# Two attention blocks on one core: the next sample's second norm on ScalarE alone, and two kinds of weight loads issued by ScalarE at set places

## The chip, the core and the metric

The kernel runs on one core of a Trainium2 chip. The time is that of one execution on the device in microseconds (us). Engines are named as the profile names them: PE is TensorE (matrix products), PEld its loading of weights, DVE is VectorE, ACT is ScalarE, POOL is GpSimd and SP is SyncE, which here only issues transfers (DMAs).

## What is computed

The input x has 8 samples of 512 channels by 1024 positions, all in float32. Two layers follow each other, and the eight samples are independent. Cut to what matters:

```python
# layer 0: group norm over 32 groups of channels, 8 heads of 64 channels
h = group_norm(x, norm_w, norm_b)
q, k, v = qkv_w @ h + qkv_b                    # each 512 x 1024 for a sample
o = softmax(q^T k * 64**-0.5) v                # for each head
x = x + proj_w @ o + proj_b
# layer 1: a norm over the whole sample, one head of 512 channels
n = (x - mean(x)) * rsqrt(var(x) + 1e-5) * gamma + beta
q, k, v = wq @ n + bq, wk @ n + bk, wv @ n + bv
x = x + wo @ (v softmax(q^T k * 512**-0.5)^T) + bo
```

## The kernel before

**Stages of a sample.** The loop over b (the 8 samples) is written out in full. For one sample PE runs these stages: the products for V of layer 0 (`make_v`, tile ps_v); the half of q and k that is still open (ps_s_qk, ps_o_qk and ps_l_qk, by `pairs_qk_twice`); the scores and values of 4 pairs of heads (s and ps_o); the first half of q and k of the *next* sample (ps_q, ps_k); the projection (ps_p); then in `attention1` the q stage (ps_q again, with the combined weights of q and k of layer 1), V of layer 1 (ps_s_v, ps_o_v and ps_l_v, by `make_v_twice`), the scores (ps_s, ps_l), and the values (ps_o at L1466, then ps_s_two and ps_o_two at L1588). The first norm of sample b+1 is thus computed while sample b is in layer 0. To hold fewer buffers its result is not kept: near the end of sample b, x of b+1 is loaded once more and normed a second time from the same scale and shift. This is the "second norm" of the title.

**Strassen's scheme.** Every large product is done by quarters in Winograd's form of Strassen's scheme (`strassen`, L414): seven products of quarters in place of eight. Sums of quarters of one side are called S1 to S4, those of the other T1 to T4. Each group of seven uses two accumulators in PSUM, one called line and one called single. Between the products, ACT copies the line (L425), and DVE adds what the results need. Where the kernel applies the scheme twice (`by_two_steps`, L526), it needs the S sums of a quarter of a weight as well. These "second-step sums of weights" are made once, written to DRAM, and later read back in two loads of 512 KB each by the class `WeightTwice` (L504 and L505): `qk_twice` for layer 0 (7 samples, b > 0) and `wvo_twice` for V of layer 1 (all 8 samples).

**The order of the work.** PE, ACT and DVE run in the order in which the program is written. A stage is a list of steps, and `at_steps` runs "hooks" after chosen steps, so that a hook's number sets where its instructions stand between the stage's own, on each engine. SP's order is not written by hand: the framework puts its transfers where it finds them due. A program counts DMAs with eight semaphores in turn, so in each queue a DMA also waits for the one eight places before it. Tiles of 512 KB come from one pool of 36 buffers (L88).

**Around the second norm.** `normed` (L366) works on 128x512 pieces, four chunks of channels in each of two halves of the positions. Odd chunks are done by ACT (`activation` with scale and bias, L372), even ones by DVE (`tensor_scalar`, L374), so a sample's second norm has four of each. It is called from `at_values` (L1719): half 0 at hook 8, half 1 at hook 9 of the values stage of layer 1. Steps 0 to 9 of this stage are `four_of(0)` and `four_of(1)` (L1554, five products each); then come the seven steps of `two_of` (L1577), whose products alternate between a line (ps_s_two) and a single (ps_o_two). After each of these DVE adds the accumulator to a sum c (L1594), and only then may PE write that accumulator again. In the order of DVE, around hooks 8 and 9, stand the quotients (L1482 and L1485), the four pieces of the norm (L374), the first two additions of c, and then in turn one of the four differences T1 to T4 of the next sample's x (`Combined.make`, L400, called t_again) and one addition of c.

**Around the loads.** `WeightTwice("wvo1")` stands at the head of `attention1` (L1219) and `WeightTwice("qk13")` at the head of V of layer 0 (L897). Both are issued by SP. In SP's order the first load of wvo_twice stands between two groups of eight small transfers (L1069, 64 KB each), which spread the reciprocals of the softmax sums over the partitions; the second stands behind the second group and a load of w_wvo. DVE multiplies by these reciprocals (`divide`, L957) ahead of the four sums T1 to T4 for the projection (L1007) and of the projection's own additions (L1180). The first load of qk_twice stands between loads of x and stores of out, the second behind these stores.

**The q stage** (`make_q`, L1234) has the steps of two groups of Strassen's scheme, one after the other in turn. On ACT it has six copies of a line (L425) and eight scaled results (L1242); two of the latter wait for the vector c, which the hook at 5 makes (`norm.untaken`, L354 to L357).

Of the kernel before, what the change touches and what calls it, by code (L numbers as in the profile page):

```python
# [46 lines left out]
P = 128  # L47
C = 512
NC = C // P
# [16 lines left out]
def two_attention_blocks(  # L66
# [17 lines left out]
    nc = tc.nc  # L84
# [112 lines left out]
    stored = {}  # L197
# [106 lines left out]
    class Norm:  # L304
# [58 lines left out]
            nc.vector.tensor_tensor(bias, made["v_b"], bias, ALU.subtract)  # L363
            return bias

        def normed(self, hs, halves=range(2)):  # L366
            for half in halves:
                for cc in range(NC):
                    h, x = piece(hs, cc, half), piece(self.xs, cc, half)
                    scale, shift = self.scale[:, cc : cc + 1], self.shift[:, cc : cc + 1]  # L370
                    if cc % 2:
                        nc.scalar.activation(h, x, AF.Identity, bias=shift, scale=scale)  # L372
                    else:
                        nc.vector.tensor_scalar(h, x, scale, shift, ALU.mult, ALU.add)  # L374
# [121 lines left out]
    class WeightTwice:  # L496
# [3 lines left out]
        def __init__(self, name, make=None):  # L500
            tiles = [flat(tile2(f"{name}_twice_{n}")) for n in range(2)]
            key, self.tiles = f"{name}_twice", tiles
            if make is None:
                nc.sync.dma_start(tiles[0], stored[key][:, : 8 * P])  # L504
                nc.sync.dma_start(tiles[1], stored[key][:, 8 * P :])  # L505
                return
            for n, pair in enumerate(PAIRS):
                for i, (a, _) in enumerate(pair):
                    sums_a(self.quarters(a, make), tiles[n][:, i * 4 * P : (i + 1) * 4 * P])
            stored[key] = dram.tile([P, 16 * P], FP, tag=key, name=f"stored_{key}")  # L510
            for n in range(2):
                nc.sync.dma_start(stored[key][:, n * 8 * P : (n + 1) * 8 * P], tiles[n])
# [85 lines left out]
    def at_steps(steps, hooks):  # L598

        n = -1  # L600
        for n, _ in enumerate(steps):
            for hook in hooks.get(n, []):
                hook()
        assert n >= max(hooks, default=-1)
# [219 lines left out]
    def pairs_qk_twice(w, twice_a, oc, bs, twice_b, qs, ks, b):  # L824

        pairs = [[tile2(f"{n}_{name}_0_{b}_{oc}") for name in "qk"] for n in ["c11", "c12"]]
        for i, ts in enumerate([qs, ks]):
            (c11, c22), (c12, c21) = ([p[i][:, half, :] for half in range(2)] for p in pairs)
            ts[oc], ts[oc + 2] = [c11, c12], [c21, c22]

        def bias(i, n):
            at = [V_BQ0, V_BK0][i] + oc + 2 * n
            return vec[:, at : at + 1]

        of = both_of(w)
        parts = twice_a.all(of)

        def multiply(bank, n, x, y, start):
            for i, (a, v) in enumerate(PAIRS[n]):
                nc.tensor.matmul(  # L840
                    bank[:, i * 2 * P : (i + 1) * 2 * P], parts[a][x], twice_b[v][y],
                    start=start and i == 0, stop=True, skip_group_check=True,
                )

        def multiply_line(i, bank, a, v, start):
            for k in range(2):
                nc.tensor.matmul(  # L847
                    bank, of(i, a)[:, k, :], bs[v][:, k, :], start=start and k == 0, stop=k == 1,
                    skip_group_check=True,
                )  # L850

        def at(n, r, t):
            return pairs[n][r][:, :, t * 2 * P : (t + 1) * 2 * P]

        return by_two_steps(multiply, multiply_line, pairs, at, bias, f"qk_0_{b}")
# [29 lines left out]
    def layer0(bs, qs, ks, b, norm_next):  # L885
# [3 lines left out]
        w = next_weight().parts[0]  # L889
        hooks = {}  # L890
# [3 lines left out]
            hooks[8] = [lambda cc=cc: norm_next.of_channels(cc) for cc in range(NC)]  # L894
        twice_b = {}
        if b > 0:
            twice_a = WeightTwice("qk13")  # L897
            for n, part in enumerate(["B21", "T1", "B22", "T4"]):
                hooks.setdefault(n, []).append(lambda part=part: twice_b.update(
                    {part: quarters_b(bs[part], f"{part}_twice_0_{b}")}  # L900
                ))
# [63 lines left out]
        w = next_weight()  # L965
# [10 lines left out]
        hooks = {8: [lambda: score(0)], 9: [lambda: score(1)]}  # L976
# [12 lines left out]
        if b == 0:  # L989
            hooks[9].append(lambda: WeightTwice("qk13", both_of(w)))  # L990
            at_steps(together(*pairs_qk(w, 1, bs, qs, ks, b)), hooks)
        else:
            hooks = {n + 10: more for n, more in hooks.items()}
            at_steps(pairs_qk_twice(w, twice_a, 1, bs, twice_b, qs, ks, b), hooks)
        xs = load_x(b, nc.sync)
        norm = norm1(xs, b)

# [137 lines left out]
        if not last:  # L1135
# [3 lines left out]
            hooks = {  # L1139
                0: [lambda n=n: combine2(n, 0) for n in range(1, 5)],  # L1140
                1: [lambda: folded(end)],
                3: [
                    lambda: sum_couple(couple, [room("sum", g) for g in range(2)]),
                    lambda: copy_couple(couple, 0), lambda: copy_couple(couple, 1),
                    lambda: one_over_couple(couple, 0),
                ],
                5: [lambda: held_couple(0)],
# [10 lines left out]
        later = []  # L1158
# [39 lines left out]
        w = next_weight().parts[0]  # L1198
# [7 lines left out]
    def attention1(xs, norm, b, at_values):  # L1206
# [9 lines left out]

        qs = quarters_of(f"q_1_{b}")
        w = next_weight().parts[0]
        twice_w = WeightTwice("wvo1")  # L1219
        combine, later = Combined(f"1_{b}"), []  # L1220
        combine.take(xs)
        bs = combine.parts
# [11 lines left out]
        def make_q(c):  # L1234
# [25 lines left out]
            6: [lambda: halve_b("T1")],  # L1260
            7: [lambda: halve_b("B22")],
            8: [lambda: halve_b("T4")],
            5: [norm.untaken, lambda: later.pop(0)(), lambda: later.pop(0)()],
        })
        bias = norm.bias()

# [5 lines left out]
        def finish_q(n):  # L1272
            q_parts[f"S{n}"] = tile2(f"s{n}_q_{b}")
            finish(q_parts, a21, n)

        at_steps(make_v_twice(w, twice_w, bs, twice_b, v_pairs, f"v_1_{b}"), {
            **{2 * n + 3: [lambda n=n: finish_q(n)] for n in range(1, 5)}, 13: [lambda: halve_a("S1")],
        })

# [354 lines left out]
    with tc.manual_schedule(engines={PE, ACT, DVE}):  # L1634
# [72 lines left out]
        for b in range(B):  # L1707
            if 0 < b < B - 1:
                ahead = [norm0(load_x(b + 1, nc.sync), b + 1)]
            xs, norm, qs, ks = layer0(bs, qs, ks, b, ahead[0] if b + 1 < B else None)  # L1710
            at_values = {}
            if b + 1 < B:

                again, combine_next = ahead[0], Combined(f"again_{b}")

                def load_again():
                    again.xs = load_x(b + 1, nc.sync)

                at_values = {  # L1719
                    2: [load_again], 8: [lambda: again.normed(again.xs, [0])],  # L1720
                    9: [lambda: again.normed(again.xs, [1])],
                    10: [lambda: combine_next.take(again.xs)],
                    **{n + 10: [lambda n=n: combine_next.make(n)] for n in range(1, 5)},
                }
                bs = combine_next.parts
            attention1(xs, norm, b, at_values)
# [412 lines left out]
```

## Time and profile before

| what | value |
|---|---|
| median of 3 runs (lowest to highest) | 2853.42 us (2852.35 to 2854.21) |
| the profiled execution's own time | 2854.65 us |
| span of the profile | 2852.4 us, granted PE clock 0.999 |
| PE busy | 2835.5 us (99%) |
| DVE busy | 2109.9 us (74%) |
| ACT busy | 1107.3 us (39%) |
| POOL busy | 220.1 us (8%) |
| DMA moved | 228.83 MB, mean 80 GB/s |
| loads of wvo_twice | 16 of 512 KB, median 5.1 us to landing |
| loads of qk_twice | 14 of 512 KB, median 6.4 us to landing |
| L374, DVE, 128x512 | 540 ns each |
| L372, ACT, 128x512 | 804 ns each |

Every figure but the first row is from one profiled execution. A busy PE is modelled: the end of a matrix product is computed, not observed. The profile's text lists waits as "who <- whom: us in total, times, longest us". A line of the timeline has the start, the duration, the engine, the source line, the operation, the tiles as out<-in, how many instructions are merged (x4), and in square brackets the idle time of the engine before it with what ended it. SPq and ACTq are the instruction queues of SP and ACT, on which DMAs are issued. A steady sample takes about 350 us; sample b = 1 begins at 413 us, when PE starts on its ps_v.

### The profile page before, as it was taken

Reading aid. Unit: us, or ns where it says so; the run is one execution under the profiler, and the core shown is the slowest. Engines: PE = TensorE matmul, PEld = TensorE weight load, DVE = VectorE, ACT = ScalarE, POOL = GpSimd, SP = SyncE. Lnnn points to the kernel's source line nnn. Section 1 sums busy time; section 2 is a strip of 40 time slices with the busy share of each in tenths; the row PEclk is TensorE's granted clock in tenths of the full one; section 3 lists DMA queues with packets and bytes.
Section 4 is the critical chain, followed back from the end, with each engine's and each line's share of the span. In section 5 each row is a group of like instructions: output and inputs, shape, how many; then the busy total and the mean of one; then the engine's idle time right before and its main releaser. Section 6 shows DMA issues by size and latency. Waiting matters only on the chain.

```text
span 2852.4 us, 37942 instructions
## 1 busy us (share of the span) xinstructions
PE 2835.5 (99%) x15200; PEld 1500.8 (53%) x15200; DVE 2109.9 (74%) x2863; ACT 1107.3 (39%) x1536; POOL 220.1 (8%) x172
## 2 busy tenths in 40 slices
PE   9999999999999999999999999999999999999999
PEld 5434765347643476435673356733557335573365
DVE  6686696866967768776677777777767777767867
ACT  3462324623256231553325523265232652326432
POOL 0000210002000030000300003000030000300011
PEclk9999999999999999999999999999999999999999
DMA  8512132121322213223132131322212222122001
GB/s 288 178 42 88 52 111 93 42 89 53 111 93 49 84 68 97 92 46 107 56 107 73 43 107 56 107 79 49 96 63 100 79 60 87 61 74 68 23 1 38
DMA packets 82567, 228.83 MB, mean 80 GB/s; under 512 B 20432, under 2 KB 21200, under 8 KB 75984
## 3 DMA queue, kind: packets, MB, share of 16 engines
q1 hardware_dynamic: 82240, 226.31, 24.7%
q8 instruction: 121, 1.98, 0.3%
q14 instruction: 62, 0.51, 0.1%
q10 hardware_dynamic: 144, 0.02, 0.0%
HBM read 153.16 MB, written 30.67 MB: 64 GB/s over the span
## 4 chain that ended last, share of the span: by engine, by line
PE 93%; DVE 5%; issue 0%; SPq 0%; ACT 0%; DMA 0%; POOL 0%; DVEq 0%; POOLq 0%
PE s L918 16%; PE ps_o L937 15%; PE ps_q L611 10%; PE ps_v L626 7%; PE ps_o L1466 7%; PE ps_p L611 6%; PE ps_s L1307 6%; PE ps_l L1323 4%; PE ps_k L611 3%; PE ps_l_v L626 3%; PE ps_s L1323 3%; PE ps_l_qk L847 3%; PE ps_s_v L868 2%; PE ps_s_qk L840 2%; PE ps_o_v L868 2%; PE ps_s_two L1588 1%
## 5 line engine op out<-in xcount | busy, mean ns | idle before, releaser
L777 ACT ACTIVATE p<-s 128x1024 f32<-128x1024 f32 x512 | 524.0, 1025 | 322.1 <-PE s L918 310.4
L779 DVE TENSOR_TENSOR acc<-acc,p 128x1024 f32<-128x1024 f32 x384 | 469.3, 1222 | 98.6 <-ACT p L777 85.8
L937 PE MATMUL ps_o<-p,v 64*64 64x512 f32 x4096 | 528.7, 589 | 0.0
L937 PEld LDWEIGHTS ps_o<-p,v 64*64 64x64 f32 x4096 | 156.6, 133 | 282.8 <-issue 278.4
L918 PE MATMUL s<-q,k 64*64 64x512 f32 x2304 | 298.5, 591 | 0.0
L918 PE MATMUL s<-c_q,c_k 64*64 64x512 f32 x1792 | 233.0, 590 | 0.0
L339 POOL TENSOR_TENSOR rstd<-rstd,minus_half 128x4 f32<-128x4 f32 (+1 forms) x16 | 19.8, 1240 | 2108.4 <-DVE rstd L338 2108.4
L918 PEld LDWEIGHTS s<-q,k 64*64 64x64 f32 x2304 | 86.3, 133 | 162.6 <-issue 156.6
L1466 PE MATMUL ps_o<-t_p,s_v 128*128 128x512 f32 x384 | 168.2, 594 | 0.0
L918 PEld LDWEIGHTS s<-c_q,c_k 64*64 64x64 f32 x1792 | 67.7, 133 | 126.3 <-issue 114.9
L779 DVE TENSOR_TENSOR acc<-p,p 128x1024 f32<-128x1024 f32 x64 | 77.9, 1217 | 73.8 <-ACT p L777 73.8
L1311 ACT COPY p<-ps_s 128x512 f32<-128x512 f32 x96 | 56.1, 585 | 195.3 <-PE ps_s L1307 193.9
L1466 PEld LDWEIGHTS ps_o<-t_p,s_v 128*128 128x128 f32 x384 | 72.3, 190 | 94.5 <-issue 94.5
L1307 PE MATMUL ps_s<-s_q,t 128*128 128x512 f32 x256 | 120.3, 592 | 0.0
L425 ACT COPY u_v<-ps_v 128x512 f32<-128x512 f32 x48 | 28.1, 586 | 231.6 <-PE ps_v L626 225.3
L1296 ACT ACTIVATE p<-p,factor 128x512 f32<-128x512 f32 (+1 forms) x112 | 86.8, 782 | 78.6 <-DVE p L1333 48.2
L611 PE MATMUL ps_p<-t_p,w_p 128*128 128x512 f32 x256 | 114.5, 596 | 2.8 <-DVE u_p L1180 2.0
L1333 DVE TENSOR_TENSOR p<-ps_s,p 128x512 f32<-128x512 f32 x88 | 60.0, 688 | 76.7 <-PE ps_s L1323 76.5
L611 PE MATMUL ps_q<-t,w_wqk 128*128 128x512 f32 x256 | 116.0, 597 | 0.0
L425 ACT COPY u_q<-ps_q 128x512 f32<-128x512 f32 x75 | 43.6, 581 | 177.1 <-PE ps_q L611 177.1
L1063 DVE RECIPROCAL inv<-inv 128x512 f32<-128x512 f32 x28 | 93.7, 3346 | 22.9 <-ACT inv L786 22.9
L1333 DVE TENSOR_TENSOR p<-ps_l,p 128x512 f32<-128x512 f32 x104 | 70.9, 688 | 47.5 <-PE ps_l L1323 47.5
(438 smaller groups left out, 4817.0 us busy)
## 6 DMA issues: line engine op xcount, KB each, us to landing
x<-in_x SPq DMA_DIRECT2D x92, 512.0 KB, 7.0
w_qk<-stored_qk SPq DMA_DIRECT2D x14, 1792.0 KB, 7.2
inv<-inv SPq DMA_DIRECT2D x248, 64.0 KB, 2.0
w_wqk<-stored_wqk SPq DMA_DIRECT2D x8, 1792.0 KB, 7.4
fold<-acc SPq DMA_DIRECT2D x56, 256.0 KB, 3.1
w_wvo<-stored_wvo SPq DMA_DIRECT2D x8, 1792.0 KB, 7.5
out<-x SPq DMA_DIRECT2D x28, 512.0 KB, 3.2
w_v<-stored_v SPq DMA_DIRECT2D x7, 1792.0 KB, 7.1
```

The costliest lines, as they stand in the source:

```text
L611: nc.tensor.matmul(bank, w[a][:, k, c * P : (c + 1) * P], bs[b][:, k, :], start=fresh and k == 0, stop=k == 1, skip_group_check=True,)
L626: nc.tensor.matmul(bank[:, u * 2 * P : (u + 1) * 2 * P], bs[b][:, k, n * P : (n + 1) * P], w[a][:, k, :], start=fresh and u == k == 0, sto ...
L777: nc.scalar.activation(p, s, AF.Exp, scale=factor)
L779: nc.vector.tensor_tensor(acc, first, p, ALU.add)
L868: nc.tensor.matmul(bank[:, (2 * i + u) * P : (2 * i + u + 1) * P], twice_b[v][y][:, u * P : (u + 1) * P], parts[a][x], start=start and i = ...
L918: nc.tensor.matmul(s[cols, j, :], ks[pair][k0 // HALF][rows, k0 % HALF : k0 % HALF + HD], qs[pair][g][rows, :], start=True, stop=True,)
L937: nc.tensor.matmul(o[cols, half, :], vs[kt][rows, c0 : c0 + HD], p[rows, j, :], start=kt == 0, stop=kt == NT - 1,)
L1063: nc.vector.reciprocal(invs[g], invs[g])
L1307: nc.tensor.matmul(bank, bs[v][:, k, t * P : (t + 1) * P], q_parts[a][:, k, :], start=a == "A11" and k == 0, stop=k == 1, skip_group_check ...
L1323: nc.tensor.matmul(bank[:, u * 2 * P : (u + 1) * 2 * P], v[y][:, u * P : (u + 1) * P], a[x], start=start and u == 0, stop=True, skip_group ...
L1333: nc.vector.tensor_tensor(at(r, t), bank, at(r, t), ALU.add)
L1466: nc.tensor.matmul(bank, v_parts[kt // 2][a][:, kt % 2, c * P : (c + 1) * P], p_parts[kt // 2][b][:, kt % 2, cols], start=fresh and kt == ...
```

## The change

Three things change. The second norm is called with `by_act=range(NC)`, so all its eight pieces are done by ACT and none by DVE, and half 0 is called at hook 7 in place of hook 8. The first norm keeps its alternation. The two loads in `WeightTwice` are issued by ACT in place of SP. And the places of both uses are set by a hook: `qk_twice` at hook 2 of V of layer 0, `wvo_twice` at hook 5 of the q stage, ahead of `norm.untaken`.

```diff
-        def normed(self, hs, halves=range(2)):
+        def normed(self, hs, halves=range(2), by_act=range(1, NC, 2)):
@@
-                    if cc % 2:
+                    if cc in by_act:
                         nc.scalar.activation(h, x, AF.Identity, bias=shift, scale=scale)
                     else:
                         nc.vector.tensor_scalar(h, x, scale, shift, ALU.mult, ALU.add)
@@ class WeightTwice
             if make is None:
-                nc.sync.dma_start(tiles[0], stored[key][:, : 8 * P])
-                nc.sync.dma_start(tiles[1], stored[key][:, 8 * P :])
+
+                nc.scalar.dma_start(tiles[0], stored[key][:, : 8 * P])
+                nc.scalar.dma_start(tiles[1], stored[key][:, 8 * P :])
                 return
@@ layer0
         if b > 0:
-            twice_a = WeightTwice("qk13")
+            twice_a = []
+            hooks[2] = [lambda: twice_a.append(WeightTwice("qk13"))]
@@
-            at_steps(pairs_qk_twice(w, twice_a, 1, bs, twice_b, qs, ks, b), hooks)
+            at_steps(pairs_qk_twice(w, twice_a[0], 1, bs, twice_b, qs, ks, b), hooks)
@@ attention1
-        twice_w = WeightTwice("wvo1")
+        twice_w = []
@@
-            5: [norm.untaken, lambda: later.pop(0)(), lambda: later.pop(0)()],
+            5: [lambda: twice_w.append(WeightTwice("wvo1")), norm.untaken, lambda: later.pop(0)(), lambda: later.pop(0)()],
@@
-        at_steps(make_v_twice(w, twice_w, bs, twice_b, v_pairs, f"v_1_{b}"), {
+        at_steps(make_v_twice(w, twice_w[0], bs, twice_b, v_pairs, f"v_1_{b}"), {
@@ the loop over samples
                 at_values = {
-                    2: [load_again], 8: [lambda: again.normed(again.xs, [0])],
-                    9: [lambda: again.normed(again.xs, [1])],
+                    2: [load_again], 7: [lambda: again.normed(again.xs, [0], range(NC))],
+                    9: [lambda: again.normed(again.xs, [1], range(NC))],
```

## Prediction

> **What bounds the kernel now.** I read the page's busy times first, then PE's waits, then the timelines of PE and DVE around the longest wait, then ACT and SP at the places where the loads go. From the page:
>
> ```profile
> PE 2835.5 (99%) x15200; PEld 1500.8 (53%) x15200; DVE 2109.9 (74%) x2863; ACT 1107.3 (39%) x1536; POOL 220.1 (8%) x172
> ```
>
> PE's waits ("who <- whom: us in total, times, longest"):
>
> ```profile
> PE ps_s_two L1588 <- DVE c L1594: 6.6, 7, 0.9
> PE ps_p L611 <- DVE u_p L1180: 2.0, 2, 1.6
> ```
>
> PE is the bound. Only its waits can be won, 11.1 us in all, and two of them bear on the change. The first is the same in all seven samples that have a next one. In the timeline of PE, and then in that of DVE:
>
> ```profile
> 402.25 1.03 PE L1588 MATMUL ps_o_two<-p,s_v 128*128 128x256 f32 x4
> 404.21 1.13 PE L1588 MATMUL ps_s_two<-B_p_twice,A_v_twice 128*128 128x256 f32 x4 [0.94 <-DVE c L1594]
> 405.18 1.03 PE L1588 MATMUL ps_s_two<-B_p_twice,S_v_twice 128*128 128x256 f32 x4
> ```
>
> ```profile
> 399.53 0.75 DVE L1485 SCALAR_TENSOR_TENSOR x<-o,bias,x 128x512 f32<-128x512 f32 x1
> 400.20 1.00 DVE L374 TENSOR_SCALAR x<-x,scale,shift 128x512 f32<-128x512 f32 x2
> 401.12 0.74 DVE L1482 SCALAR_TENSOR_TENSOR o<-ps_o,rstd,inv 128x512 f32<-128x512 f32 x1
> 401.90 0.75 DVE L1485 SCALAR_TENSOR_TENSOR x<-o,bias,x 128x512 f32<-128x512 f32 x1
> 402.56 1.00 DVE L374 TENSOR_SCALAR x<-x,scale,shift 128x512 f32<-128x512 f32 x2
> 403.48 0.68 DVE L1594 TENSOR_TENSOR c<-ps_s_two,c 128x512 f32<-128x512 f32 x1
> ```
>
> PE may reuse the accumulator ps_s_two only after DVE's first addition of c (ends 404.16), and DVE is late because four pieces of the norm (L374) stand ahead of it. The accumulator itself was ready at about 401.6 (the second of its two groups starts at 400.52 and takes 1.03).
>
> The stall is larger than the 0.94 us shown. Groups of four matmuls start 0.86 us apart when nothing waits. After 402.25 the next should start at 403.11, but starts at 404.21 (1.10 late), and the one after it follows 0.97 later (0.11 more). So it costs 1.20 us.
>
> The second wait shows in the windows from one sample's ps_v to the next:
>
> ```profile
> 413.12:764.12 351.00, 349.41 (x1885) 185.67 (x1885) 262.52 (x352) 136.83 (x188) 28.23 (x21) 1.00 0.25 79
> 1114.40:1464.62 350.22, 349.12 (x1886) 185.75 (x1885) 262.51 (x352) 136.81 (x188) 28.22 (x21) 1.00 0.25 79
> 2165.09:2517.35 352.26, 349.40 (x1885) 185.67 (x1885) 262.69 (x352) 136.83 (x188) 28.22 (x21) 1.00 0.23 74
> ```
>
> The first column is the length. A steady sample takes 350.22; b = 1 has 0.78 more and b = 6 has 2.04 more. In both, DVE's division (L957) waited for the small reciprocal transfers (L1069), and PE for the additions queued behind it.
>
> **What the Trainium skill says.** "Perfetto Trace Analysis", section "DMA Instruction — HWDGE (DVE, Sync)": the issuing engine's sequencer itself waits for the DMA's semaphores and makes its descriptors, and is only then free for its next instruction. The trace agrees in kind: SP's 512 KB issues take 0.53 and 0.45 us. The same page, section "DVE / Act Engine Instruction (TENSOR_ADD, Activation, etc)": a compute instruction is pushed to a wait queue, after which the sequencer takes the next one. So a DMA behind a waiting copy could issue during that wait; no row of before shows this on ACT. "DMA: Bandwidth & Descriptors", section "Issuing engines are not separate DMA queues": transfers of all issuers share the same DMA engines. The trace agrees: reciprocal transfers ahead of the wvo_twice load land in 2.0 us, those behind it in up to 4.1 to 5.1.
>
> **Part 1: the norm leaves DVE.** Removed from DVE: four L374 for each of 7 samples. Two take 400.20 to 401.12 and two 402.56 to 403.48, so 1.84 us ahead of the first addition of c. Without them that addition starts at 401.65 (403.48 - 1.84), just after its accumulator is ready, and ends at 402.33, 0.78 ahead of PE's 403.11. The second addition can start at 403.3, after ps_o_two ends, and is needed at 404.8. From there each 1.73 us step of PE has one addition and one difference t_again on DVE, 1.74 us, as before, and DVE keeps its 0.8 us of slack. What is next: V of layer 0 needs the accumulators released by the last addition of c (ends at 415.5 before, needed at 416.4); both move forward by about 1.1 to 1.2 us. So the whole stall goes: 7 x 1.20 = 8.4 us.
>
> Added on ACT: four L372 a sample. Four take 2.93 us with 0.80 each, so 0.71 apart; eight take 5.8. In ACT's timeline:
>
> ```profile
> 393.06 2.93 ACT L372 ACTIVATE x<-x,shift,scale 128x512 f32<-128x512 f32 x4
> 395.89 0.62 ACT L786 ACTIVATE held_inv<-inv 128x512 f32<-128x512 f32 x1
> 414.88 0.59 ACT L425 COPY u_v<-ps_v 128x512 f32<-128x512 f32 x1 [18.29 <-PE ps_v L626]
> ```
>
> They follow the same two copies as before, whether at hook 7 or 8, and end at 398.9. The first difference t_again needs them at about 403.9, ACT's next urgent work is at 413.7: cost nothing. If the 5 us cover were gone, DVE would wait in front of t_again, with the additions of c behind it.
>
> **Part 2: loads leave SP.** In SP's timeline of b = 1:
>
> ```profile
> 592.60 0.53 SPq L504 DMA_DIRECT2D wvo_twice<-stored_wvo_twice  x1
> 593.33 5.65 SPq L1069 DMA_DIRECT2D inv<-inv  x8
> ```
>
> Without L504 the second group of reciprocals issues up to 0.73 us earlier (in b = 6 only 0.45, as DVE's reciprocal ends at 2345.3), no 512 KB transfer is ahead of it, and its last member no longer waits for that load, which was the eighth DMA before it. So b = 1 loses its 0.78. In b = 6 one small DMA took 2.12 us to issue against the usual 0.59, and another had been slow before the load was issued, so the load need not be the cause: at least 0.45, at most 2.04. I take 0.5. Together 1.3 us, bounds 0 and 2.8. The qk_twice loads leave SP where PE waits for nothing: nothing. POOL keeps its order.
>
> **Part 3: loads arrive on ACT.** The q stage is the tight place:
>
> ```profile
> 285.49 0.59 ACT L425 COPY u_q<-ps_q 128x512 f32<-128x512 f32 x1 [1.35 <-PE ps_q L611]
> 286.17 1.52 ACT L1242 ACTIVATE q<-u_q,c,vec 128x512 f32<-128x512 f32 x2
> 287.60 0.56 ACT L425 COPY u_q<-ps_q 128x512 f32<-128x512 f32 x1
> ```
>
> Both DMAs come between the first copy and the L1242s. Their DMA semaphores belong to reciprocal transfers landed some 40 us before. If the sequencer runs ahead, they issue during the copy's 1.35 us wait, which covers 0.53 + 0.45 = 0.98: cost zero. If they start only when the copy ends (286.08), the L1242s move from 286.17 to 287.06, 0.89 later, and the third copy ends at 289.05 instead of 288.16. PE needs that bank at 283.49 + 3 x 1.72 = 288.65, so it stands 0.40, with 0.25 for restarting as above 0.65, 8 times: 5.2 us. A gain is excluded, since ACT only gets work. I take zero, by the skill's wait queue. Landing: issued by 287.1, the slowest load of before (8.4) lands at 295.5; PE reads it at 299.2.
>
> For qk_twice the DMAs stand between copies at 418.33 and 425.24, a hole of 6.3 us, and their other waits (two stores of out, one DVE quotient at 401.9) are over by about 407: nothing. Landing at 420 + 9.1 = 429 against first use at 440.6. The engine moves as many bytes as before.
>
> **The sum.** Profiled execution: span 2852.4 - 8.4 - 1.3 = 2842.7, with 2.25 outside the span 2844.95. The shown median is 1.23 below this execution's own time; 2853.42 - 9.7 = 2843.7.
>
> **Rivals.**
> - A, as above: 2843.7, chance 0.55.
> - B, the reciprocal waits stay, because the slow issues are random: 2853.42 - 8.4 = 2845.0, chance 0.20. For it: the slow issue in b = 6; against: 2.0 us landings ahead of the load.
> - C, ACT's DMAs wait for the copy: 2843.7 + 5.2 = 2848.9, chance 0.12.
> - D, the change of the norm doesn't do what it says, since a late t_again or quotient becomes PE's wait in V: 2853.42 - 1.3 = 2852.1, chance 0.07. Against: the slack of 0.8 us above, and 5 us on ACT.
> - E, slower: ACT's issue in the q stage is dearer than SP's. With d per DMA the loss is 8 x (2d - 0.09 - 0.49 + 0.25), which eats 9.7 us from d = 0.77. SP's qk_twice issues took 0.87 and 0.73 in the median, so 1.0 isn't absurd: 13.4 lost, 2857.1, chance 0.06.
>
> **How the numbers follow.** About 0.2% (5.7 us) can be told from no change. Below 2847.7 lie A, B and a little of C: faster 0.77. Same: the rest of C and D, 0.17. Slower 0.06. The range reaches from A with all of b = 6 (2853.42 - 8.4 - 2.8 = 2842.2, and a little spread) to nearly all of C: 2842.0 to 2848.5.
>
> **What the new profile would show.** Part 1 right: no wait of ps_s_two for c, and 8 L372 in a row ending before 399. Part 2: second reciprocal groups landing in 2.0 us, no ps_p wait. Part 3: ACTq slices of L504 that start before the second copy ends, and no wait of PE for u_q in the q stage; a PE wait there of 0.4 us, 8 times, is C, and over 1 us is E. I am wrong if PE's samples don't shorten from 350.2 to 349.0.

## The result, and the profile after

The changed kernel takes 2843.86 us in the median (2843.32 to 2844.74, seven runs), the kernel before in the same runs 2853.92 us: a ratio of 0.9965, with a 95% interval of 0.9954 to 0.9977, so about 10 us or 0.35% less. The profiled execution took 2844.74 us, its span is 2843.0 us, 9.4 us shorter than the span of before. Lines of the code from L505 on have a number one higher than before, and from about L899 on two higher: the additions of c, L1594 before, are L1596, and the wvo_twice and qk_twice loads are L505 and L506.

From the page, busy time of each engine:

```profile
PE 2834.0 (100%) x15200; PEld 1501.4 (53%) x15200; DVE 2094.7 (74%) x2835; ACT 1125.5 (40%) x1564; POOL 220.0 (8%) x172
```

DVE has 28 instructions less and ACT 28 more: four pieces in seven samples. PE's waits ("who <- whom: us in total, times, longest"), the whole list:

```profile
PE ps_warm L1643 <- POOL in_sample L163: 1.2, 1, 1.2
PE ps_p L612 <- DVE u_p L1182: 0.5, 1, 0.5
PE ps_p L612 <- DVE inv L791: 0.5, 1, 0.5
```

The seven waits of ps_s_two for c are gone. Of the two waits of ps_p for u_p one is left, in sample 1. The five waits of ps_s_two for o, 0.2 us each, have left the list too, but not the kernel: the group behind them still takes 0.97 us to the next one (400.02 to 400.99), as it did before (399.55 to 400.52). The place of the long wait, in PE's timeline and then in DVE's (start, length, instruction, idle time before it):

```profile
402.71 1.03 PE L1590 MATMUL ps_o_two<-p,s_v 128*128 128x256 f32 x4
403.58 1.03 PE L1590 MATMUL ps_s_two<-B_p_twice,A_v_twice 128*128 128x256 f32 x4
404.44 1.03 PE L1590 MATMUL ps_s_two<-B_p_twice,S_v_twice 128*128 128x256 f32 x4
```

```profile
401.45 0.75 DVE L1487 SCALAR_TENSOR_TENSOR x<-o,bias,x 128x512 f32<-128x512 f32 x1
402.12 0.68 DVE L1596 TENSOR_TENSOR c<-ps_s_two,c 128x512 f32<-128x512 f32 x1
403.78 0.69 DVE L1596 TENSOR_TENSOR c<-ps_o_two,c 128x512 f32<-128x512 f32 x1 [0.98 <-PE ps_o_two L1590]
```

PE's groups now start 0.87 and 0.86 us apart. The first addition ends at 402.80, 0.78 us before PE needs its accumulator, and now DVE waits for PE (0.98 us) and not PE for DVE. ACT, which took over the pieces:

```profile
393.53 5.75 ACT L372 ACTIVATE x<-x,shift,scale 128x512 f32<-128x512 f32 x8
...
414.14 0.58 ACT L425 COPY u_v<-ps_v 128x512 f32<-128x512 f32 x1 [14.24 <-PE ps_v L627]
```

Windows from one sample's ps_v to the next (first column after the colon pair: length), samples 1, 3 and 6:

```profile
412.37:762.31 349.94, 349.13 (x1886) 185.75 (x1885) 260.43 (x348) 139.49 (x192) 28.20 (x21) 1.00 0.25 79
1111.37:1460.38 349.01, 348.86 (x1886) 185.84 (x1885) 260.35 (x348) 139.41 (x192) 28.22 (x21) 1.00 0.25 79
2158.77:2507.82 349.05, 348.86 (x1885) 185.75 (x1885) 260.42 (x348) 139.49 (x192) 28.21 (x21) 1.00 0.23 73
```

A steady sample went from 350.22 to 349.01, by 1.21 us. In sample 3 PE comes to its first ps_s_two 336.66 us after the sample's start in both kernels, so all of it lies behind that point. Sample 6 fell by 3.21. Sample 1, 351.00 before, still has 0.93 more than a steady one.

On SP, the reciprocals of sample 1 are now one piece, and nothing stands between the groups:

```profile
586.78 11.73 SPq L1071 DMA_DIRECT2D inv<-inv  x16
598.61 0.53 SPq L212 DMA_DIRECT2D w_wvo<-stored_wvo  x1
```

On ACT, in the q stage of sample 0 (ACTq lines are issues of DMAs):

```profile
285.97 0.58 ACT L425 COPY u_q<-ps_q 128x512 f32<-128x512 f32 x1 [1.35 <-PE ps_q L612]
285.97 0.34 ACTq L505 DMA_DIRECT2D wvo_twice<-stored_wvo_twice  x1
286.35 0.44 ACTq L506 DMA_DIRECT2D wvo_twice<-stored_wvo_twice  x1
286.92 1.52 ACT L1244 ACTIVATE q<-u_q,c,vec 128x512 f32<-128x512 f32 x2 [0.37 <-DVE factor L357]
288.34 0.56 ACT L425 COPY u_q<-ps_q 128x512 f32<-128x512 f32 x1
```

The first load starts within 0.01 us of the copy, in all eight samples: not during the copy's 1.35 us wait, and not after its end. The scalings start 0.95 us after the start of the copy, where it was 0.68 before. The bracket names DVE's factor, which ends at 286.74, but before the scalings started 0.10 us ahead of the end of factor (286.17 against 286.27), so they don't need it. The vector c was ready at 286.61; what ends last here is the issue of the second load, at 286.79.

Where the 9.4 us of the two profiled executions lie follows from the starts of ps_v in the chain of work that ended last. The table also has the two halves of the change alone and the best version, which are told below (us, from one start of ps_v to the next):

| piece | before | after | norm alone | loads alone | reciprocals split |
|---|---|---|---|---|---|
| up to the first ps_v | 60.35 | 60.78 | 59.81 | 59.88 | 59.64 |
| sample 0 | 352.77 | 351.59 | 351.54 | 352.81 | 351.36 |
| sample 1 | 351.00 | 349.94 | 349.83 | 350.91 | 348.76 |
| sample 2 | 350.28 | 349.06 | 349.05 | 350.28 | 348.77 |
| sample 3 | 350.22 | 349.01 | 349.00 | 350.22 | 348.76 |
| sample 4 | 350.18 | 349.02 | 348.97 | 350.22 | 348.77 |
| sample 5 | 350.29 | 349.37 | 349.08 | 350.76 | 348.77 |
| sample 6 | 352.26 | 349.05 | 349.56 | 350.27 | 348.76 |
| the rest | 335.05 | 335.18 | 335.26 | 335.15 | 335.11 |

Seven times 1.2 is 8.4 of the 9.4; 2.0 more come from sample 6; 0.14 and 0.28 are given back in samples 1 and 5, and 0.56 in the start and the rest, which the change doesn't touch.

### The profile page after: what moved, and what is told of

The parts are those of the page before. It is cut to its first block, busy times and chain, and to the rows that moved or that the text cites. A ratio compares the mean times of both kernels' runs of the same rounds, so it can differ in the third digit from the quotient of the medians.

```text
span 2843.0 us, 37924 instructions
## 1 busy us (share of the span) xinstructions
PE 2834.0 (100%) x15200; PEld 1501.4 (53%) x15200; DVE 2094.7 (74%) x2835; ACT 1125.5 (40%) x1564; POOL 220.0 (8%) x172
## 4 chain that ended last, share of the span: by engine, by line
PE 95%; DVE 4%; issue 0%; SPq 0%; ACT 0%; DMA 0%; POOL 0%; DVEq 0%; POOLq 0%
PE s L920 16%; PE ps_o L939 15%; PE ps_q L612 10%; PE ps_v L627 7%; PE ps_o L1468 7%; PE ps_p L612 6%; PE ps_s L1309 6%; PE ps_l L1325 4%; PE ps_k L612 3%; PE ps_l_v L627 3%; PE ps_s L1325 3%; PE ps_l_qk L848 3%; PE ps_s_v L869 2%; PE ps_s_two L1590 2%; PE ps_s_qk L841 2%; PE ps_o_v L869 2%
```

## The experiments

The theory was that of the prediction: the norm gives 8.4 us by one stall, the loads about 1.3 us by shorter reciprocal waits, and their issue on ACT is hidden. The after profile had already put two questions: why sample 1 kept its excess, and what hides the issue if not the wait. Ratios are to the kernel before in the same series of runs.

| kernel | median, us | ratio | 95% interval |
|---|---|---|---|
| changed kernel | 2843.86 | 0.9965 | 0.9954 to 0.9977 |
| norm alone | 2844.52 | 0.9969 | 0.9956 to 0.9981 |
| loads alone | 2852.92 | 0.9997 | 0.9989 to 1.0006 |
| one half of the norm | 2846.25 | 0.9974 | 0.9965 to 0.9984 |
| four issues in the q stage | 2851.49 | 0.9992 | 0.9984 to 1.0001 |
| loads one place earlier | 2844.03 | 0.9964 | 0.9951 to 0.9978 |
| loads late on SP | 2844.37 | 0.9965 | 0.9951 to 0.9978 |
| eight copies more on ACT | 2844.68 | 0.9967 | 0.9955 to 0.9979 |
| sixteen copies more on ACT | 2851.02 | 0.9989 | 0.9981 to 0.9998 |
| eight DMAs more on SP | 2844.32 | 0.9967 | 0.9954 to 0.9980 |
| sixteen DMAs more on SP | 2844.88 | 0.9968 | 0.9957 to 0.9980 |
| reciprocals split | 2841.39 | 0.9956 | 0.9943 to 0.9970 |

**The norm alone.** To the changed kernel, both pairs of loads go back:

```diff
-                nc.scalar.dma_start(tiles[0], stored[key][:, : 8 * P])
-                nc.scalar.dma_start(tiles[1], stored[key][:, 8 * P :])
+                nc.sync.dma_start(tiles[0], stored[key][:, : 8 * P])
+                nc.sync.dma_start(tiles[1], stored[key][:, 8 * P :])
...
-            twice_a = []
-            hooks[2] = [lambda: twice_a.append(WeightTwice("qk13"))]
+            twice_a = [WeightTwice("qk13")]
...
-        twice_w = []
+        twice_w = [WeightTwice("wvo1")]
```

> The kernel before with the norm's part of the change alone: ACT takes all eight pieces of the next sample's second norm; both pairs of loads stay with SP at their places of before. My theory: the stall of PE for the first addition of c goes, 1.20 us in each of seven samples, so 8.4 us less than before (ratio 0.9971), and no wait of PE's ps_s_two for c is left; the second groups of reciprocals still land in 4 to 5 us. Rival: the gain came from the loads, and this part alone gives 1 to 2 us (ratio 0.9995), because a later addition or difference takes over the wait.

2844.52 us, 9.0 less than the 2853.49 of before; by the table steady samples lose 1.2 each. No wait of ps_s_two for c is left. The rival falls: this part is nearly all of the change. And sample 6, whose loads stand where they stood, lost 2.7 of its 352.26: 1.2 by the norm and 1.5 by nothing that was changed.

What the loads do to the reciprocals shows in sample 2, which is steady. DVE's and SP's timelines of this kernel, with the load between the groups:

```profile
938.02 3.34 DVE L1065 RECIPROCAL inv<-inv 128x512 f32<-128x512 f32 x1
...
946.43 0.69 DVE L959 TENSOR_TENSOR o<-o,inv 128x512 f32<-128x512 f32 x1 [0.36 <-DMA inv<-inv]
947.90 0.69 DVE L959 TENSOR_TENSOR o<-o,inv 128x512 f32<-128x512 f32 x1 [0.78 <-DMA inv<-inv]
```

```profile
935.58 4.98 SPq L1071 DMA_DIRECT2D inv<-inv  x8
940.66 0.53 SPq L505 DMA_DIRECT2D wvo_twice<-stored_wvo_twice  x1
941.39 4.94 SPq L1071 DMA_DIRECT2D inv<-inv  x8
```

and the same of the changed kernel, without it:

```profile
939.15 3.35 DVE L1065 RECIPROCAL inv<-inv 128x512 f32<-128x512 f32 x1
...
947.12 0.68 DVE L959 TENSOR_TENSOR o<-o,inv 128x512 f32<-128x512 f32 x1
949.05 0.69 DVE L959 TENSOR_TENSOR o<-o,inv 128x512 f32<-128x512 f32 x1 [1.25 <-DMA inv<-inv]
```

```profile
936.72 10.75 SPq L1071 DMA_DIRECT2D inv<-inv  x16
```

The last division starts 12.32 us after the first small DMA with the load (947.90 - 935.58), and 12.33 without it (949.05 - 936.72). The load was issued in a gap: SP has sent the first eight and waits for DVE's second reciprocal, which ends at 941.36 here, and the second eight start at 941.39. The load delays the landing of some of the small DMAs (up to 4.4 us, 2.0 without it), but the last one still lands about 2 us after it is issued, and the last division waits for that one. The load, which is the eighth DMA ahead of that last one, doesn't hold it up either: the last DMA takes 0.59 us to issue with the load and without it.

**The loads alone.** To the changed kernel, the norm goes back to hooks 8 and 9 with DVE taking half:

```diff
-                    2: [load_again], 7: [lambda: again.normed(again.xs, [0], range(NC))],
-                    9: [lambda: again.normed(again.xs, [1], range(NC))],
+                    2: [load_again], 8: [lambda: again.normed(again.xs, [0])],
+                    9: [lambda: again.normed(again.xs, [1])],
```

> The kernel before with the loads' part of the change alone: both pairs of loads are issued by ACT at the new places, the norm is shared between DVE and ACT as before. My theory: the seven waits of ps_s_two for c stay at 0.94 us; the second groups of reciprocals land in 2.0 us; ps_p's waits shrink; 1.3 us less than before, at most 2.8 (ratio 0.9990 to 1.0000). Rival: one of the small DMAs of samples 1 and 6 is slow to issue for a reason of its own, so that their waits stay in part and the gain is under 0.7 us. A second rival: the issue on ACT in the q stage costs 0.4 us or more eight times, and the kernel gets slower by 2 us or more.

2852.92 us, 0.57 less, an interval that holds no change. PE's longest wait is that of before:

```profile
PE ps_s_two L1590 <- DVE c L1596: 6.6, 7, 0.9
```

The sixteen small DMAs land in at most 2.7 us in samples 2 to 5, in up to 3.9 in sample 1 and 3.7 in sample 6, and by the table every sample but 6 is within 0.1 us of before or longer. So the small gain, if it is one, is the first rival's: the traces differ where a small DMA happened to be slow. The two halves together, 9.0 and 0.6, make the changed kernel's 10.1 within what can be told.

**One half of the norm.**

```diff
-                    9: [lambda: again.normed(again.xs, [1], range(NC))],
+                    9: [lambda: again.normed(again.xs, [1])],
```

> The changed kernel, but of the second norm ACT takes all of the first half only; in the second half two pieces go back to DVE, 0.92 us ahead of c's first addition. My theory: what counts is the point at which that addition ends. In the changed kernel it ends 0.78 us before PE needs it, so 0.92 us more makes it 0.14 us late, which costs 0.15 to 0.3 us with the restart, seven times: 1 to 2 us slower than the changed kernel (ratio to before 0.9968 to 0.9973). Rival: each piece on DVE costs its time, so half of the gain goes: 4.2 us slower than the changed kernel (ratio to before 0.9980).

2846.25 us, 2.4 more than the changed kernel; steady samples 349.3 to 349.4 instead of 349.0. DVE and PE:

```profile
402.24 1.00 DVE L374 TENSOR_SCALAR x<-x,scale,shift 128x512 f32<-128x512 f32 x2
403.16 0.68 DVE L1596 TENSOR_TENSOR c<-ps_s_two,c 128x512 f32<-128x512 f32 x1
```

```profile
402.84 1.03 PE L1590 MATMUL ps_o_two<-p,s_v 128*128 128x256 f32 x4
403.90 1.13 PE L1590 MATMUL ps_s_two<-B_p_twice,A_v_twice 128*128 128x256 f32 x4
404.87 1.03 PE L1590 MATMUL ps_s_two<-B_p_twice,S_v_twice 128*128 128x256 f32 x4
```

PE starts 0.20 late and loses 0.11 more at the next group: 0.31 a sample, 2.2 in seven. A quarter of the gain is lost and not half, so the deadline theory holds; it was 0.4 us above the upper end of what was expected. The addition ends at 403.84, 0.14 late as forecast; PE starts 0.06 after that end, and the next group loses its 0.11 however short the wait is. The last 0.2 us of the 2.4 can't be told from noise. This wait carries no mark in the timeline and stands in no list of waits. Only the distance between starts shows it.

**Four issues in the q stage.** Each wvo_twice load is cut in two:

```diff
-                nc.scalar.dma_start(tiles[0], stored[key][:, : 8 * P])
-                nc.scalar.dma_start(tiles[1], stored[key][:, 8 * P :])
+                cuts = 4 if name == "wvo1" else 2
+                for i, n in enumerate(range(0, 16, 16 // cuts)):
+                    nc.scalar.dma_start(
+                        tiles[n // 8][:, n % 8 * P : (n % 8 + 16 // cuts) * P],
+                        stored[key][:, n * P : (n + 16 // cuts) * P])
```

> The changed kernel with each of the two loads that ACT issues in the q stage cut into two, so four DMAs of half the size at the same place. My theory: the issue is on ACT's path, and only the 0.23 us left ahead of PE's next use of the copied bank hides it. Four issues of about 0.38 us from the start of the second copy move the two scalings 0.76 us later and make the third copy 0.5 us late, 0.8 us with the restart, eight times: 6 us slower than the changed kernel (ratio to before 0.9986). Rival: the issue runs beside ACT's instructions, and nothing moves (ratio to before 0.9965).

2851.49 us, 7.6 more than the changed kernel. PE's waits and ACT's timeline:

```profile
PE ps_q L613 <- ACT u_q L425: 4.4, 8, 0.6
```

```profile
285.90 0.59 ACT L425 COPY u_q<-ps_q 128x512 f32<-128x512 f32 x1 [1.35 <-PE ps_q L613]
285.90 1.78 ACTq L507 DMA_DIRECT2D wvo_twice<-stored_wvo_twice  x4
287.81 1.52 ACT L1245 ACTIVATE q<-u_q,c,vec 128x512 f32<-128x512 f32 x2 [1.32 <-issue]
289.23 0.56 ACT L425 COPY u_q<-ps_q 128x512 f32<-128x512 f32 x1
```

Four issues take 1.78 us, the scalings start 1.91 after the copy, and the stall of 0.55 shown costs the steady sample 349.83 - 349.02 = 0.81, as expected. Eight of them are 6.5; sample 3 has another 0.8 in the reciprocals' stage, and sample 1 has 1.1, close to its excess in the changed kernel. A load of half the size is no cheaper to issue: the four take 0.33 and three times 0.44 us. So the issue is on ACT's path, and only a small slack hides it.

**Loads one place earlier.** The two loads stand between the two copies instead of behind the second:

```diff
-            4: [norm.deviation, lambda: combine.make(4)],
+            4: [lambda: twice_w.append(WeightTwice("wvo1")), norm.deviation, lambda: combine.make(4)],
...
-            5: [lambda: twice_w.append(WeightTwice("wvo1")), norm.untaken, lambda: later.pop(0)(), lambda: later.pop(0)()],
+            5: [norm.untaken, lambda: later.pop(0)(), lambda: later.pop(0)()],
```

> The changed kernel with ACT's two loads in the q stage one place earlier in its queue: between the two copies of u_q that start 1.94 us apart, ahead of the second one instead of behind it. My theory: ACT takes its instructions in order, a load starts when the instruction ahead of it has started; the loads now start at about 284.0 with the earlier copy, are issued by 284.9, inside the second copy's wait of 1.35 us, and the two scalings start 0.68 us after the second copy instead of 0.95. The time stays that of the changed kernel within 0.5 us, as the 0.27 us was hidden there too. Rival, which the prediction held: the sequencer goes on while a copy waits, and the loads start up to 6.5 us ahead of the earlier copy, at 277.5 to 283.

2844.03 us, the changed kernel's time. ACT's timeline:

```profile
282.88 0.58 ACT L425 COPY u_q<-ps_q 128x512 f32<-128x512 f32 x1 [6.50 <-PE ps_q L612]
282.89 0.34 ACTq L505 DMA_DIRECT2D wvo_twice<-stored_wvo_twice  x1
283.27 0.44 ACTq L506 DMA_DIRECT2D wvo_twice<-stored_wvo_twice  x1
284.82 0.58 ACT L425 COPY u_q<-ps_q 128x512 f32<-128x512 f32 x1 [1.35 <-PE ps_q L612]
285.51 1.52 ACT L1244 ACTIVATE q<-u_q,c,vec 128x512 f32<-128x512 f32 x2
```

The copy ahead waited 6.50 us, and the load started 0.01 us after it, though it had nothing of its own to wait for: issued by SP, in the next experiment, it starts at 271.93. Here the issue lies inside the second copy's wait, and the scalings are back at 0.69 after the copy. That is the cover the prediction had in mind; it needs the loads one place earlier than the change puts them.

**Loads late on SP.** The new places in the program, but the old engine: only `nc.scalar.dma_start` becomes `nc.sync.dma_start` in the two lines of the loads.

> The changed kernel with the loads at their new places in the program, but issued by SP. On SP they then stand behind the second group of reciprocals and the load of w_v, and behind the second pair of stores. My theory: it is the place that frees the reciprocals, not the engine: second groups land in 2.0 us as in the changed kernel, loads land before PE reads them, and the time is that of the changed kernel within 0.5 us (ratio to before 0.9965). Rival: a load behind SP's waiting instructions comes late, and PE waits for wvo_twice or qk_twice, 1 us or more in each sample: 8 us slower than the changed kernel.

2844.37 us with a ratio of 0.9965: the changed kernel's. SP issues the loads at 271.93 and 272.45, they land by 282.2, long before PE's first use at 299.3, and the q stage on ACT is that of before (scalings 0.69 after the copy). Which engine issues the loads doesn't matter here.

**More work behind the norm on ACT.** Eight and sixteen copies of pieces onto themselves (`padded` is called with 1 and with 2):

```diff
-                    9: [lambda: again.normed(again.xs, [1], range(NC))],
+                    9: [lambda: again.normed(again.xs, [1], range(NC)), lambda: padded(again.xs, 1)],
...
+                def padded(xs, times):
+                    for n in range(times * 2 * NC):
+                        h = piece(xs, n // 2 % NC, n % 2)
+                        nc.scalar.copy(h, h)
```

> The changed kernel with eight copies of a piece onto itself by ACT behind the norm's eight activations (values unchanged), 4 to 6 us more. My theory: the cover of the norm on ACT is some 5 us, as the first difference t_again, which reads the pieces, starts at 404.4 and DVE has another 0.8 to 1 us of slack there; the copies end at 403 to 405 and cost less than 1.5 us in all (ratio to before 0.9965 to 0.9970). Rival: the norm on ACT is already at its limit, because something else waits behind it, and each us on ACT shows in the time: 28 us or more.

> The changed kernel with sixteen copies of a piece onto itself by ACT behind the norm's eight activations (values unchanged). My theory: at 0.48 to 0.70 us each they end at 407 to 410.5, which is 2.6 to 6 us after t_again could start; the additions of c queued behind it on DVE come late, PE gets a wait of ps_s_two or ps_o_two for c again, of 1.5 to 5 us in each of seven samples: 10 to 35 us slower than the changed kernel, so slower than before (ratio 1.000 to 1.009). Rival: the scheduler's order lets c's additions pass, and the cost stays under 2 us.

Eight copies end at 403.15 and cost nothing that can be told: 2844.68 us, steady samples 349.0 to 349.1. Sixteen end at 406.3 and cost 7.2 us, about 1.07 us a steady sample. DVE of the second kernel:

```profile
402.47 0.69 DVE L1596 TENSOR_TENSOR c<-ps_o_two,c 128x512 f32<-128x512 f32 x1 [0.98 <-PE ps_o_two L1590]
404.22 1.22 DVE L400 TENSOR_TENSOR t_again<-x,x 128x1024 f32<-128x1024 f32 x1 [1.06 <-ACT x L1721]
405.37 0.68 DVE L1596 TENSOR_TENSOR c<-ps_s_two,c 128x512 f32<-128x512 f32 x1
406.30 1.23 DVE L400 TENSOR_TENSOR t_again<-x,t_again 128x1024 f32<-128x1024 f32 x1 [0.25 <-ACT x L1721]
```

The mechanism is the expected one, t_again late with additions of c behind it, and PE waits for c again (1.5 us shown in seven). The size was missed: 10 to 35 us were expected. The copies were 0.53 us apart and not up to 0.70, and t_again takes the pieces one after the other, so that the first two differences waited 1.06 and 0.25 us and the later ones not at all. The cover on ACT thus lies between the 4.25 us of eight copies, which cost nothing, and the 8.40 us of sixteen; the 5 us of the prediction are in this range.

**Is the slow small DMA bound to its place in SP's queue?** Eight and sixteen small DMAs that nobody reads are added in sample 0:

```diff
+            for n in range(8):
+                nc.sync.dma_start(unread[:, n : n + 1], vectors[:, n : n + 1])
```

> The changed kernel with eight DMAs of one column of the vectors each, into a tile that nothing reads, added to SP's queue in sample 0. In the runs so far one of the sixteen reciprocal DMAs of sample 1, and one of sample 6, took 1.0 to 1.9 us to issue instead of 0.59: the twelfth or thirteenth of sample 1 where both loads are off that place, the fifteenth in both kernels that have a load there. My theory: the slow issue is bound to a place in SP's own stream of instructions, so eight more DMAs move it to an earlier one of the sixteen (about the fourth) in sample 1 and out of the group in sample 6. Rival: it is bound to the moment (some 594 to 597 and 2335 to 2346 us into the span), and stays the twelfth or thirteenth. The time stays that of the changed kernel within 1 us either way.

> As with eight added DMAs, but sixteen. My theory: the slow issue leaves the sixteen reciprocals of sample 1 (and of sample 6), sample 1 loses its excess of 0.9 us over a steady sample, and ps_p's wait for u_p there goes, unless another sample gets a slow issue in their place. Rival: nothing moves, sample 1 keeps its wait of 0.3 to 0.8 us.

The theory falls: in both kernels it is the twelfth DMA of sample 1 (1.56 and 1.44 us) and the sixth of sample 6 (1.31 and 1.30). The rival, put as a moment, isn't shown either: between these two kernels the DMA moved from 593.61 to 594.66, by the 1.05 us by which its group moved. In the kernels with a load between the groups it is the fifteenth of sample 1 (1.29 and 1.35 us), in the others the twelfth or thirteenth. So it goes with the place in the program, but not with SP's own count.

The traces hold what goes with it. Among the DMA queues the page of the changed kernel counts one of the kind "instruction" (packets, MB, share):

```profile
q8 instruction: 121, 1.98, 0.3%
```

By its name it brings the program's own instructions. Its packets are of 16 KB, and the traces have the time of each. In the changed kernel one runs from 594.32 to 595.61, and the slow issue of sample 1 from 594.40 to 595.98. In the 13 traces together 104 issues of inv<-inv take over 0.9 us. 103 of them overlap such a packet and end 0.24 to 0.43 us after it. The other is the 2.12 us of sample 6, in the profile of before alone; it overlaps a packet of 1.95 us on a second instruction queue (q14), whose packets otherwise take at most 0.87. Of the 3329 issues that overlap no instruction packet the longest takes 0.86. PE and PEld have 30400 instructions for 121 packets, some 250 for each (an estimate); if the packets are PE's, they follow PE's progress, which fits that DMAs added on SP don't move them. No run moved a packet on purpose: this is a coincidence in time, though one without exception, and how a packet holds up an issue isn't shown.

The slow issue accounts for the excess of sample 1. In the changed kernel its last division starts 13.22 us after its first small DMA, against 12.33 in sample 2: 0.89 of the 0.93.

**Reciprocals split between SP and ACT.** If SP's issue of the last eight sets the last division, half of them should go elsewhere:

```diff
-        def one_over_couple(couple, g):
-            nc.vector.reciprocal(invs[g], invs[g])
-            for n, pair in enumerate(couple):
+        def one_over_couple(couple, g, ns=range(2), queue=nc.sync):
+            if 0 in ns:
+                nc.vector.reciprocal(invs[g], invs[g])
+            for n in ns:
+                pair = couple[n]
...
-                        nc.sync.dma_start(
+                        queue.dma_start(
...
-                6: [lambda: one_over_couple(couple, 1)],
+                6: [lambda: one_over_couple(couple, 1, [0])],
...
-                8: [lambda: held_couple(1)],
+                8: [lambda: one_over_couple(couple, 1, [1], nc.scalar), lambda: held_couple(1)],
```

> The changed kernel with the last four of the sixteen reciprocal DMAs of each sample issued by ACT, ahead of its copy held_inv that waits for the same reciprocal. My theory: what is left of ps_p's waits (0.9 us in sample 1, 0.3 in sample 5) is the length of SP's issue of these sixteen DMAs, so with twelve on SP and four on ACT at once the last lands some 2.5 us earlier and both excesses go: 1.2 us less than the changed kernel (ratio to before 0.9960). Rival: ACT's four issues, about 1.6 us, hold up the scaling of k behind them and PE waits for its bank: slower than the changed kernel by 0.5 us or more a sample, 4 us in all.

2841.39 us (2840.54 to 2841.78), ratio 0.9956: the best kernel of the study, 2.5 us under the changed one, whose runs (from 2843.32) don't overlap with it. Twice what was expected. DVE's last two divisions of sample 2 stand without a wait:

```profile
944.57 1.28 DVE L959 TENSOR_TENSOR o<-o,inv 128x512 f32<-128x512 f32 x2
```

The last one starts 11.00 us after the first small DMA, 12.33 in the changed kernel. ACT's four issues take 2.5 to 2.7 us a sample and 3.98 in sample 1, more than the 1.6 of the rival, and in sample 2 the scaling of k starts 1.2 us later; but PE doesn't wait for it. In sample 1 the slow issue is now on ACT's queue, its fourth (593.32 to 595.20, with an instruction packet from 593.39 to 594.81), and costs nothing any more.

Samples 1 to 6 are now of one length, and a steady one lost another 0.25 to 0.29. That was a stall in every sample that the list of waits doesn't hold. It is to be seen in the changed kernel's weight loads (PEld) of sample 2:

```profile
955.03 0.30 PEld L612 LDWEIGHTS ps_p<-t_p,w_p 128*128 128x128 f32 x2 [0.86 <-DVE u_p L1182]
```

PE's matmuls of t_p start 0.43 us apart, but here the step is 0.63 (954.40 to 955.03), because DVE's addition of u_p ends at 954.97; the 28 matmuls of t_p up to the next group take 12.31 us in the changed kernel (953.12 to 965.43), 12.02 in this one (950.57 to 962.59).

## Why the prediction was right, and where it was not

**What bounds the kernel.** Right: PE, by the waits named. But the list of waits was taken as all that can be won. It isn't: each sample held 0.25 to 0.29 us more in the stage of ps_p, as a step that is too long and as an idle time of the weight loads.

**Part 1, 8.4 us.** Right in mechanism, place and size. The stall of 0.94 shown was worth 1.20: steady samples fell by 1.21. The first addition of c was to end 0.78 us before PE needs it, and does; ACT's eight pieces were to take 5.8 us and take 5.75. "Ending before 399" became 399.28, in an execution in which everything is 0.43 later from the start on. The next deadline, V, showed no wait. The cover of 5 us on ACT was tested by the copies: eight hide, sixteen don't.

**Part 2, 1.3 us.** The mechanism failed. The step was "the second group of reciprocals issues up to 0.73 us earlier", and with it "b = 1 loses its 0.78". DVE's timeline of before has, in sample 1:

```profile
589.96 3.34 DVE L1063 RECIPROCAL inv<-inv 128x512 f32<-128x512 f32 x1
```

It ends at 593.30, and the second group needs it: the prediction allowed for this end in b = 6 but not in b = 1. So the group starts 5.80 us after the first with the load (593.33 - 587.53) and without it, and the load lay in that gap. The landings fell as foreseen, in the steady samples from over 4 us to 2.0; this agrees with the Trainium skill's "DMA: Bandwidth & Descriptors", section "Issuing engines are not separate DMA queues", as far as it goes: SP issued both, so transfers of two issuers weren't compared. But these were not the last ones that DVE waits for. Sample 1 kept its excess (0.93 instead of 0.78): one of its small DMAs is slow to issue in every kernel, always beside an instruction packet. What sample 6 gave, 2.0 us of this profile, was one slow DMA of one execution, of which the runs with the norm alone gave 1.5 back without any load moved. As to the waits, rival B described it; its 2845.0 and A's 2843.7 are too close for the runs to choose: the sum of the steps came out near 10 us because the norm alone measured 9.0 and the loads 0.6, neither of which can be told from 8.4 and 0. That the median lies within 0.2 us of A is luck.

**Part 3, nothing.** Right in the cost, wrong in the reason. The step was that "the sequencer runs ahead" and the loads issue during the copy's 1.35 us wait, by the Trainium skill's "Perfetto Trace Analysis", section "DVE / Act Engine Instruction (TENSOR_ADD, Activation, etc)". Here the loads start when the waiting copy starts (285.97 and 285.97, and 282.89 against 282.88 behind a wait of 6.50 us): in this case the measurement decides against that reading. Rival C's other reading, that they start when the copy ends, is wrong as well. Most of the issue (0.58 of 0.78 us) overlaps the copy; what sticks out moves the scalings by 0.27 and the third copy to 288.90, while PE needs its bank at 288.65 + 0.48 = 289.13, by the prediction's own rule and this execution's later start. So 0.23 us were left, and the zero was a near thing: with two issues more it costs 0.81 a sample. Rival E's price of 0.77 us per DMA was far off, at 0.34 and 0.44; in the V stage the second qk_twice load took up to 0.75, and its hole of 6.3 us held it.

## What to carry to other kernels

A wait ends at a deadline: work out how far behind it the last instruction ends, take away that much, and see what stands next. What is taken away beyond that, and work that is moved out of a gap, gives nothing. To judge whether moving a DMA ahead of others helps, ask first what the others waited for: here an engine's result, and then the length of the issue on one queue, which for the last eight went from 4.94 to 2.73 us when two queues shared it. Look for PE's stalls in the distances between its groups too, since a stall of 0.3 us in every sample stood in no list of waits.

## What was not expected of the hardware

- A DMA on ACT behind a copy that waits for PE starts when that copy starts, and runs beside it: 285.97 with 285.97, 282.89 with 282.88.
- The price of an issue isn't one number. A 512 KB load took 0.34 and 0.44 us on ACT in the q stage, 0.53 and 0.45 on SP before, 0.42 and 0.38 on SP in the later place. Loads of 256 KB took the same 0.33 and 0.44 on ACT. Four 64 KB DMAs took 2.5 to 2.7 us on ACT in the last experiment, 0.54 to 0.86 each, against 0.59 each on SP, and 3.98 in sample 1, where one took 1.88.
- One small DMA of a certain sample is slow to issue, 1.2 to 1.9 us against 0.59, at a place that eight or sixteen added DMAs on its own queue don't move. In every trace it overlaps a packet of the instruction queue q8 and ends 0.24 to 0.43 us after that packet; how the one holds up the other isn't shown. The cause of the 0.2 to 0.5 us by which sample 5 exceeds a steady one in some of the kernels was not found.
